# Layer 1's quartered aggregates in a two-layer graph network: where T's subtractions, the left-over banks, the running sums and the background work stand

## The chip, the cores and the metric

The kernel runs on one core of one Trainium2 chip. The metric is the device time of a whole execution in microseconds; lower is better. The times of the kernel before are 3061.73, 3063.74 and 3067.88 us, with a median of 3063.74 us.

## The reference

Two graph layers, each on 2708 nodes with 1024 features, in float32. A layer normalizes the rows, weighs every pair of nodes, masks the weights with the adjacency matrix, takes a softmax over each row and applies it to the features:

```python
h = jnp.maximum(_layernorm(x, axis=-1), 0.0)               # both layers
# layer 0
e = jax.nn.relu((h @ Wf + bf) @ (h @ Wg + bg).T)
x = x + softmax(where(adj > 0, e, NEG), axis=1) @ (h @ W + bW)
# layer 1
hw = h @ W1
e = leaky_relu(hw @ a1 + (hw @ a2).T, 0.2)
x = x + relu(softmax(where(adj > 0, e, NEG), axis=1) @ hw)
```

## The kernel before

**Panels.** The 2708 columns of the attention matrix are cut into five panels of 576, 576, 532, 512 and 512 columns (`width`). For each panel and layer, the kernel makes weights (exponentials, with a running sum `sm` over the tiles), then an *aggregate* (features times weights) and then a *project* (times W, plus the residual). Twenty tiles of 128 rows form ten pairs; one more full tile, MONO, and one of 20 rows, TINY, are left over.

**Fewer products.** Matrix products are done by a Strassen-like scheme with seven products instead of eight, named M1, M5, M6, M7, M3, M2 and M4. In layer 1, panels 1 to 4 use it twice, one inside the other (`aggregate_quartered`): the outer loop runs over the seven m in the order of `BY_QUARTERS` (M1, M5, M2, M6, M7, M3, M4), called *stages* here, and in each stage seven inner *products* follow. An inner product (`product`) is 10 matmuls, which the trace shows as 20 records, since each float32 matmul leaves two; a *pass* below is one such record. The right-hand operands are sums and differences that VectorE (DVE) makes: `make(m)` writes 20 "quarter" tiles for a stage, `fifth` writes the ten T tiles (which M5's stage uses), `second` and `fourth` rewrite the weights in place.

**PSUM banks.** A stage has the banks X, Z and Y (gx, gz, gy in the trace). The order of the products is X by M1; M4 of the stage before into that stage's Z (the closure `left_out`); Z by M6; Y by M5; X by M2; Z by M7; Y by M3. Between two products into one bank, DVE or ScalarE (ACT) has to read the bank: the second product into Z waits for `add(c12, Z, c21)`. In M2, M3 and M4 the left-over tiles follow (`left_over`, with a fourth bank U), and M7 has a *corner*, which is a `left_over` into four fresh banks. `left_over` first runs MONO's eight matmuls over all 128 rows (line 1101), then TINY's eight (line 1106). TINY's four banks use four different groups of 32 rows (`g`), with 20 rows filled in each.

**Background.** Work for later is put in lists (`later`, `lazy`) and taken up by `behind(us)`, which adds `us` to a credit and starts entries while the credit is positive. An entry of layer 1's weights is charged 2.1 us; it makes one tile of weights (ACT, two DVE operations, ACT's exponential) and adds the tile of `LAG` entries before to the sum. `exps_until(n)` forces the entries up to n. Layer 1 has 22 tiles, so there are 24 entries. The weights of the next panel are put in the list after the stage M6 and run through the rest of the aggregate and the project.

**Order.** Semaphores and the order in an engine's queue come from the framework's scheduler: an engine's instructions need not stand in the order in which they are written, except for those that are held in program order. DVE's are not held in layer 1's aggregates (`nc.hold` is empty there). Each engine then runs its own queue in order. DMA loads go through SyncE in program order.

The lines that the steps below touch: `exps, LAG` at 884, `second` in `aggregate` at 917, `quarters_of` at 1006 and after, `product` with its `behind(fine)` at 1068 to 1088, `left_over` at 1093 to 1107, `with_second`, the stage loop, and `weights1`. All DVE and ACT helpers are recorded under line 45, so their instructions are told apart by tile names: `V` or `gT` is the target of a bank's add, `T` of `fifth`, `quarter` of `make`, `P` and `sm` of the weights.

Of the kernel before, what the change touches and what calls it, by code (L numbers as in the profile page):

```python
# [57 lines left out]
def kernel(  # L58
# [155 lines left out]
    def behind(us, psum_free=False):  # L214
        credit[0] = min(credit[0] + us, 2 * us)
        while later and credit[0] > 0 and (psum_free or not later[0][3]) and (not later[0][4] or later[0][4]()):
            credit[0] -= one()
        while spare[0] and not later and lazy and credit[0] > 0:
            credit[0] -= one(lazy)
# [661 lines left out]
            nc.vector.reciprocal(r[:, o:o + w // 2], ps)  # L881
        return r

    exps, LAG = [0], 2

    def sums_until(n):
        while summed[0] < n:
# [2 lines left out]
    def exps_until(n):  # L890
        while exps[0] < n:
            one()
# [8 lines left out]
    def aggregate(l, p, S, sm, then={}, rate=3.0):  # L901
# [13 lines left out]
            sub(t1(q), wa_(q)[:, hi], wa_(q)[:, lo])  # L915

        def second():
            exps_until(2 * NQ + 2 + LAG)
            for q in range(NQ):
                sub(wa_(q)[:, hi], wb_(q)[:, hi], wa_(q)[:, hi])  # L920
            for q in range(NQ):
                sub(wa_(q)[:, lo], wb_(q)[:, hi], t1(q))
# [136 lines left out]
    def aggregate_quartered(p, S, sm, of_right, then={}, fine=1.2):  # L1059

        w = width[p]
        h = w // 2
        hb = h // 2
        lo, hi = slice(0, h), slice(h, w)
        G = both("gT")
        quad = lambda e, s: G[e].rearrange("p (c i) -> p c i", c=NH)[:, :, s]
        make, inner_right = of_right["make"], of_right["right"]
        lasts = {}  # L1070

        def product(m, n, ps, start):
            quarters_until(m)
            if (m, 0) not in lasts:
                for i, of in enumerate((hr_d[:, m, :, :, NK - 1].rearrange("p h f c -> p (h f) c"), hs2_d[:, m, :, NK - 1])):
                    lasts[m, i] = stream("hl2", (P, 4, WH))
                    load(lasts[m, i], of)
            t = stream("hc2", (P, NK - 1, WH))
            raw = n in (M1, M2, M4)
            i = {M1: 0, M2: 1, M4: 3, M6: 0, M3: 1, M7: 2, M5: 3}[n]  # L1080
            load(t, hr_d[:, m, i // 2, i % 2, :NK - 1] if raw else hs2_d[:, m, i, :NK - 1])
            last = lasts[m, int(not raw)][:, i]
            for k in range(NK):
                for d in range(2):
                    lhs = t[:, k] if k < NK - 1 else last
                    nc.tensor.matmul(ps[:, d], lhs[:, d * P:(d + 1) * P], inner_right(m, n, k),  # L1086
                                     start=(start and k == 0 and d == 0), stop=(k == NK - 1), skip_group_check=True)
            behind(fine)

        def bank2(name):  # L1090
            return bank(name)[:, :2 * hb].rearrange("p (d i) -> p d i", d=2)

        def left_over(banks, e, s, fresh):

            two = stream("hl", (P, W + 2 * P))
            load(two, hgl_d[1][:, e])
            cols = lambda b: slice(s.start + b * hb, s.start + (b + 1) * hb)
            for (a, b), ps in banks.items():
                for d in range(2):
                    c = 2 * a + d  # L1100
                    nc.tensor.matmul(ps[:, d], two[:, c * P:(c + 1) * P], S[MONO][:, cols(b)],
                                     start=((a, b) in fresh and d == 0), stop=False, skip_group_check=True)
            for d in range(2):
                for (a, b), ps in banks.items():
                    g = slice(B32 * (2 * a + b), B32 * (2 * a + b) + NY)
                    nc.tensor.matmul(ps[:, d], two[g, W + d * P:W + (d + 1) * P], S[TINY][g, cols(b)], start=False, stop=True,
                                     skip_group_check=True)

        inverse = []
        done_with = {M2: (0, lo), M7: (1, hi), M3: (0, hi), M4: (1, lo)}  # L1110

        def scale(m, r):
            if m in done_with:
                e, s = done_with[m]
                o = quad(e, s)[:, 2 * r:2 * r + 2]
                nc.vector.tensor_tensor(o, o, inverse[0][:, s].rearrange("p (o i) -> p o i", o=1).to_broadcast([P, 2, h]), OP.mult)

        place = {M1: [(1, lo)], M5: [(0, hi)], M2: [(0, lo)], M6: [(0, hi), (1, lo)], M7: [(1, hi), (1, lo)], M3: [(0, hi)],
                 M4: [(1, lo)]}
        direct = {M1: (0, lo), M5: (0, hi)}  # L1120
        more_of = {M2: (0, lo), M3: (0, hi), M4: (1, lo)}

        def into_place(m, V, r):
            for e, s in place[m]:
                o = quad(e, s)[:, 2 * r:2 * r + 2]
                if m == M1:
                    nc.scalar.copy(o, V[r])
                elif m == M5:
                    add(o, o, quad(0, lo)[:, 2 * r:2 * r + 2])
                else:  # L1130
                    add(o, V[r], o)

        def corner():

            four = {(a, b): bank2("gu") for a in range(2) for b in range(2)}
            left_over(four, 1, hi, four)
            for (a, b), ps in four.items():
                at = lambda e: quad(e, slice(h + b * hb, h + (b + 1) * hb))[:, 2 * a:2 * a + 2]
                add(at(1), ps, at(0))

        def with_second():
            exps_until(2 * NQ + 2 + LAG)
            make(M2)

        before_next = {M1: lambda: make(M5), M5: with_second, M2: lambda: (of_right["fourth"](), make(M6)), M6: lambda: make(M7),
                       M7: lambda: make(M3), M3: lambda: make(M4)}
        left_out = None
        for m in BY_QUARTERS:
            V = [quad(*direct[m])[:, 2 * r:2 * r + 2] for r in range(2)] if m in direct else [v[:, :, :h] for v in in_pairs("V")]
            c11, c12 = (V[0][:, :, b * hb:(b + 1) * hb] for b in range(2))  # L1150
            c21, c22 = (V[1][:, :, b * hb:(b + 1) * hb] for b in range(2))
            X = bank2("gx")
            product(m, M1, X, True)
            nc.scalar.copy(c21, X)
            if m == M1:
                of_right["fifth"]()
            if left_out:
                left_out()
            Z = bank2("gz")
            product(m, M6, Z, True)  # L1160
            add(c12, Z, c21)
            Y = bank2("gy")
            product(m, M5, Y, True)
            add(c22, Y, c21)
            if m == M7:
                corner()
            if m in before_next:
                before_next[m]()
            product(m, M2, X, False)
            if m not in more_of:  # L1170
                nc.scalar.copy(c11, X)
            product(m, M7, Z, False)
            add(c22, Z, c22)
            product(m, M3, Y, False)
            if m in more_of:
                U = bank2("gu")
                left_over({(0, 0): X, (0, 1): Y, (1, 0): Z, (1, 1): U}, *more_of[m], [(1, 1)])
                nc.scalar.copy(c11, X)
            add(c12, Y, c12)
            if m in more_of:  # L1180
                add(c22, U, c22)
            into_place(m, V, 0)
            scale(m, 0)

            def left_out(m=m, V=V, Z=Z, c21=c21):
                product(m, M4, Z, False)
                add(c21, Z, c21)
                into_place(m, V, 1)
                scale(m, 1)
            if m == M5:  # L1190
                of_right["second"]()
            if m == M5:
                inverse.append(inverse_sums(p, sm))
            if m in then:
                then[m]()
        left_out()
        return [t.rearrange("p (c i) -> p c i", c=NH) for t in G]

# [561 lines left out]
    def weights1(p, z, m, shift):  # L1760
# [16 lines left out]
        def go(i, mk):  # L1777
            if i < len(order):
# [13 lines left out]
                    nc.vector.scalar_tensor_tensor(s, ub[:n, :w], f[1][:n, t:t + 1], s, op0=OP.add, op1=OP.max)  # L1792
                    add(s, s, mk[0][:n, :w])
                nc.scalar.activation(s, s, AF.Exp)
            if i >= LAG:
                q, k = order[i - LAG]
                total(p, sm, S[units[q][k]], once(q, k), i == LAG)
            exps[0] += 1

        front = []  # L1800
        for i in range(len(order) + LAG):
            mk = []
            front.append([2.1, (lambda i=i, mk=mk: mk.append(load_mask(p, *order[i])))
                          if i < len(order) and not (p == 0 and units[order[i][0]][order[i][1]] in before) else None,
                          (lambda i=i, mk=mk: go(i, mk)), False, None])
# [92 lines left out]
```

## Time and profile before

| | |
|---|---|
| median of the runs | 3063.74 us (3061.73 to 3067.88) |
| the profiled execution | 3062.58 us, of which the span is 3060.8 us |
| TensorE matmuls (PE) | 2992.6 us busy, 98% of the span |
| VectorE (DVE) | 2041.7 us, 67% |
| ScalarE (ACT) | 546.0 us, 18% |
| GpSimd (POOL) | 496.2 us, 16% |
| DMA | 251 GB/s over the span |
| granted TensorE clock | 0.994 |

The span is what the instructions of the profiled execution cover. The four quartered aggregates lie at about 2333 to 2470 us (panel 1), 2532 to 2659 (panel 2), 2715 to 2837 (panel 3) and 2885 to 3007 (panel 4). A line of a timeline has the start and the length in us, the engine, the line of the kernel, the operation, target and sources, and, in brackets, the idle time before it and what ended it.

### The profile page before, as it was taken

What the parts mean: (1) busy time and instruction counts of PE and PEld (TensorE: products, weight loads), DVE (VectorE), ACT (ScalarE), POOL (GpSimd) and SP (SyncE); (2) the same over time, 40 slices, a digit from 0 to 9 for tenths busy, and PEclk for the clock granted to TensorE, in tenths of its full rate; (3) what the DMA queues carried; (4) which work ended last, traced back from release to release, by engine and by line L of the source; (5) the groups of instructions that cost most, each with busy time, mean ns of one, the idle gap of its engine ahead of it and who ended that gap; (6) DMA issues with size and microseconds to landing.
All of it is one profiled execution on the core that took longest, in us unless ns stands there. A gap on an engine that the chain in (4) does not pass through costs nothing.

```text
span 3060.8 us, 41690 instructions
## 1 busy us (share of the span) xinstructions
PE 2992.6 (98%) x14630; PEld 2293.3 (75%) x14630; DVE 2041.7 (67%) x4577; ACT 546.0 (18%) x887; POOL 496.2 (16%) x770
## 2 busy tenths in 40 slices
PE   8998999999999999999999999998999999999999
PEld 4576777657877588885888886784767959879695
DVE  5766794575741586616975266867878768887863
ACT  3420020021200121101211011202222121222200
POOL 1421111210112110214111111131212010020201
PEclk9999999999999999999999999998999999999999
DMA  6989978888466786757967588688767768878787
GB/s 228 302 257 270 300 278 304 264 270 242 158 234 157 225 248 228 246 156 243 296 196 248 165 233 274 229 294 322 249 199 254 270 204 299 285 270 295 256 302 269
DMA packets 448065, 766.80 MB, mean 251 GB/s; under 512 B 175488, under 2 KB 262304, under 8 KB 447824
## 3 DMA queue, kind: packets, MB, share of 16 engines
q1 hardware_dynamic: 387696, 584.80, 59.9%
q0 software_dynamic: 54464, 164.78, 16.2%
q10 hardware_dynamic: 5696, 14.55, 1.4%
q8 instruction: 116, 1.90, 0.2%
q14 instruction: 93, 0.76, 0.1%
HBM read 630.04 MB, written 138.11 MB: 251 GB/s over the span
## 4 chain that ended last, share of the span: by engine, by line
PE 71%; issue 11%; DVE 9%; DMA 4%; POOL 2%; SPq 1%; ACT 1%; POOLq 0%; DVEq 0%; ACTq 0%
PE gy L673 7%; PE gx L673 6%; PE gz L673 6%; PE sz L1397 6%; PE gz L1086 5%; PE pz L1286 4%; PE px L1286 4%; PE sx L1397 4%; PE sy L1397 3%; PE py L1286 3%; PE gy L1086 3%; PE gx L1086 3%; PE M_ps L586 3%; PE gv L673 2%; PE qz L673 2%
## 5 line engine op out<-in xcount | busy, mean ns | idle before, releaser
L1397 PE MATMUL sz<-B,As 128*128 128x288 f32 (+2 forms) x1200 | 292.1, 392 | 4.6 <-DVE st L45 4.5
L1397 PEld LDWEIGHTS sz<-B,As 128*128 128x128 f32 x1200 | 227.6, 190 | 53.7 <-DVE st L45 8.0
L1397 PE MATMUL sx<-B,As 128*128 128x288 f32 (+2 forms) x800 | 201.5, 395 | 14.2 <-DMA As<-hs_d 11.9
L1397 PE MATMUL sy<-B,As 128*128 128x288 f32 (+2 forms) x800 | 199.1, 392 | 0.4 <-DMA As<-hs_d 0.4
L1397 PEld LDWEIGHTS sx<-B,As 128*128 128x128 f32 x800 | 152.4, 191 | 48.4 <-DMA As<-hs_d 10.4
L673 PE MATMUL gz<-Sa,hc 128*128 128x288 f32 (+2 forms) x800 | 185.8, 392 | 0.0
L673 PEld LDWEIGHTS gz<-Sa,hc 128*128 128x128 f32 x800 | 151.5, 190 | 32.2 <-issue 1.8
L1397 PEld LDWEIGHTS sy<-B,As 128*128 128x128 f32 x800 | 151.7, 190 | 31.4 <-DMA As<-hs_d 0.9
L1086 PE MATMUL gz<-quarter,hc 128*128 128x128 f32 (+2 forms) x1344 | 168.8, 279 | 3.8 <-DVE gT L45 3.7
L1086 PEld LDWEIGHTS gz<-quarter,hc 128*128 128x128 f32 x1344 | 160.6, 191 | 5.1 <-DVE gT L45 4.5
L143 POOL DMA_DIRECT2D out_dram<-x_res x164 | 81.0, 500 | 466.9 <-DVE x_res L45 456.2
L1286 PE MATMUL py<-w,ps 128*128 128x512 f32 x320 | 142.5, 593 | 0.4 <-DMA w<-wt_d 0.4
L1286 PE MATMUL px<-w,gT 128*128 128x512 f32 x320 | 141.2, 593 | 1.5 <-ACT pt L45 1.5
L1286 PE MATMUL pz<-w,ps 128*128 128x512 f32 x320 | 142.1, 594 | 0.0
L143 POOL DMA_DIRECT2D mk_d<-mask x55 | 35.9, 653 | 511.5 <-DVE mask L45 505.4
L673 PE MATMUL gy<-T,hc 128*128 128x288 f32 (+2 forms) x480 | 113.6, 398 | 3.8 <-DMA hc<-hg_d 3.8
L1286 PEld LDWEIGHTS pz<-w,ps 128*128 128x128 f32 x320 | 60.2, 190 | 76.2 <-issue 70.3
L1286 PEld LDWEIGHTS py<-w,ps 128*128 128x128 f32 x320 | 60.4, 190 | 75.8 <-issue 72.3
L1286 PEld LDWEIGHTS px<-w,gT 128*128 128x128 f32 x320 | 60.1, 190 | 72.9 <-issue 67.1
L586 PE MATMUL M_ps<-wgT,wfT 128*128 128x512 f32 x256 | 111.8, 593 | 1.6 <-ACT hsT L45 1.6
L673 PEld LDWEIGHTS gy<-T,hc 128*128 128x128 f32 x480 | 92.2, 192 | 24.3 <-DMA hc<-hg_d 4.3
L45 ACT ACTIVATE P<-P 128x576 f32<-128x576 f32 (+2 forms) x110 | 71.9, 654 | 207.5 <-DVE P L45 207.4
(384 smaller groups left out, 5820.6 us busy)
## 6 DMA issues: line engine op xcount, KB each, us to landing
hc<-hg_d SPq DMA_DIRECT2D x175, 512.0 KB
As<-hs_d SPq DMA_DIRECT2D x150, 512.0 KB
hc<-hr_d SPq DMA_DIRECT2D x119, 512.0 KB
hc<-hs_d SPq DMA_DIRECT2D x112, 512.0 KB
w<-wt_d SPq DMA_DIRECT2D x96, 512.0 KB
w<-in_L_gnn_W_dram SPq DMA_DIRECT2D x72, 512.0 KB
md<-md_d SPq DMA_DIRECT2D x56, 512.0 KB
adj_i<-in_adj_dram SPq DMA_DIRECT2D x200, 128.0 KB
```

What stands on the lines that cost most here:

```text
L45: i = f(*a, **k)
L143: nc.gpsimd.dma_start(a, b)
L586: nc.tensor.matmul(ps, wfT[a][c // NH][:, c % NH, :], wgT[b][c], start=(c == 0), stop=(c == NC - 1))
L673: nc.tensor.matmul(ps[d], left(m, k, d), right(m, k), start=(start and k == 0), stop=(k == K - 1), skip_group_check=True)
L1086: nc.tensor.matmul(ps[:, d], lhs[:, d * P:(d + 1) * P], inner_right(m, n, k), start=(start and k == 0 and d == 0), stop=(k == NK - 1), ski ...
L1286: nc.tensor.matmul(ps, left[i][m][:, k, :], w_[k], start=(start and k == 0), stop=(k == NH - 1), skip_group_check=True)
L1397: nc.tensor.matmul(ps[:n, :h], lefts[q][:, i % 2, c, :n], B[m][c // 2][:, c % 2, :h], start=(start and c == 0), stop=(c == NH - 1), skip_g ...
```

## The change

There are four parts.

- **T's subtractions.** `of_right["fifth"]()` moves, in stage M1, from behind X's copy to behind Y's first add.
- **Bank Z last.** `left_over` handles its first three banks (MONO, then TINY), and then the fourth (MONO, then TINY). In the stages M2, M3 and M4 the fourth is Z. The corner goes through the same function and is split in the same way.
- **Sums.** In layer 1, weights are summed four entries behind instead of two (`LAG1`), so that there are 26 entries. Panel 0's plain aggregate takes part.
- **Background.** `behind(fine)` moves from the end of `product` to behind the copy or add that empties the bank, at all seven products of a stage.

```diff
-    exps, LAG = [0], 2
+    exps, LAG, LAG1 = [0], 2, 4
...
         def second():
-            exps_until(2 * NQ + 2 + LAG)
+            exps_until(2 * NQ + 2 + (LAG1 if l else LAG))
...
                     nc.tensor.matmul(ps[:, d], lhs[:, d * P:(d + 1) * P], inner_right(m, n, k),
                                      start=(start and k == 0 and d == 0), stop=(k == NK - 1), skip_group_check=True)
-            behind(fine)
...
-            for (a, b), ps in banks.items():
+            parts = list(banks.items())
+            for some in (parts[:3], parts[3:]):
+              for (a, b), ps in some:
                 for d in range(2):
                     c = 2 * a + d
                     nc.tensor.matmul(ps[:, d], two[:, c * P:(c + 1) * P], S[MONO][:, cols(b)],
                                      start=((a, b) in fresh and d == 0), stop=False, skip_group_check=True)
-            for d in range(2):
-                for (a, b), ps in banks.items():
+              for d in range(2):
+                for (a, b), ps in some:
                     g = slice(B32 * (2 * a + b), B32 * (2 * a + b) + NY)
...
         def with_second():
-            exps_until(2 * NQ + 2 + LAG)
+            exps_until(2 * NQ + 2 + LAG1)
             make(M2)
...
             nc.scalar.copy(c21, X)
-            if m == M1:
-                of_right["fifth"]()
+            behind(fine)
             if left_out:
                 left_out()
             Z = bank2("gz")
             product(m, M6, Z, True)
             add(c12, Z, c21)
+            behind(fine)
             Y = bank2("gy")
             product(m, M5, Y, True)
             add(c22, Y, c21)
+            if m == M1:
+                of_right["fifth"]()
+            behind(fine)
...
             if m not in more_of:
                 nc.scalar.copy(c11, X)
+            behind(fine)
             product(m, M7, Z, False)
             add(c22, Z, c22)
+            behind(fine)
             product(m, M3, Y, False)
             if m in more_of:
                 U = bank2("gu")
-                left_over({(0, 0): X, (0, 1): Y, (1, 0): Z, (1, 1): U}, *more_of[m], [(1, 1)])
+                left_over({(0, 0): X, (0, 1): Y, (1, 1): U, (1, 0): Z}, *more_of[m], [(1, 1)])
                 nc.scalar.copy(c11, X)
             add(c12, Y, c12)
...
             scale(m, 0)
+            behind(fine)
 
             def left_out(m=m, V=V, Z=Z, c21=c21):
                 product(m, M4, Z, False)
                 add(c21, Z, c21)
                 into_place(m, V, 1)
                 scale(m, 1)
+                behind(fine)
...
-            if i >= LAG:
-                q, k = order[i - LAG]
-                total(p, sm, S[units[q][k]], once(q, k), i == LAG)
+            if i >= LAG1:
+                q, k = order[i - LAG1]
+                total(p, sm, S[units[q][k]], once(q, k), i == LAG1)
...
-        for i in range(len(order) + LAG):
+        for i in range(len(order) + LAG1):
```

## Prediction

> **What bounds the kernel.** I read the page first: busy shares, then who waited for whom, then the queues of PE and DVE around each wait.
>
> ```profile
> span 3060.8 us, 41690 instructions
> PE 2992.6 (98%) x14630; PEld 2293.3 (75%) x14630; DVE 2041.7 (67%) x4577; ACT 546.0 (18%) x887; POOL 496.2 (16%) x770
> ...
> PE gz L1101 <- DVE V L45: 4.5, 3, 2.2
> PE gz L1086 <- DVE gT L45: 3.7, 3, 1.4
> ```
>
> PE is the bound, so time comes back only where PE stands still, and every pass added to PE is paid in full. The last two lines are the answer on waits for engine PE (total us, times, longest): they are all that PE waits in the four quartered aggregates. The change can gain little more than these 8.2 us. The first wait is in stage M3 of panels 1, 2 and 3 (2.17, 1.19 and 1.15 us in the PE timeline), where bank Z's MONO matmuls wait for the add that empties Z. The second is in stage M1 of panels 2, 3 and 4 (1.39, 1.14, 1.14), where the second product into Z waits for Z's first add. This is DVE's and PE's queue at the M1 wait of panel 2:
>
> ```profile
> 2537.84 0.42 DVE L45 TENSOR_TENSOR T<-P 128x266 f32<-128x266 f32 x1
> 2538.78 3.18 DVE L45 TENSOR_TENSOR T<-P 128x266 f32<-128x266 f32 x9
> 2541.89 0.42 DVE L45 TENSOR_TENSOR gT<-gz,gT 128x266 f32<-128x266 f32 x1
> 2543.69 0.42 DVE L45 TENSOR_TENSOR gT<-gy,gT 128x266 f32<-128x266 f32 x1
> ...
> 2551.55 3.53 DVE L45 TENSOR_TENSOR P<-P,T 128x266 f32<-128x266 f32 x10
> 2555.70 0.42 DVE L45 TENSOR_TENSOR gT<-gz,gT 128x266 f32<-128x266 f32 x1
> ...
> 2542.36 2.08 PE L1086 MATMUL gz<-quarter,hc 128*128 128x133 f32 x16 [1.39 <-DVE gT L45]
> ```
>
> All ten T subtractions stand ahead of Z's add. Note also that `second` (P<-P,T) stands ahead of adds of stage M5 that are written before it: the queue is ordered by what the scheduler takes to be ready, not as written. Now the left-over matmuls, PE's timeline in panel 3, stages M2 and M7:
>
> ```profile
> 2760.90 0.37 PE L1106 MATMUL gx<-P,hl 20*128 20x128 f32 x1
> 2760.91 0.37 PE L1106 MATMUL gy<-P,hl 20*128 20x128 f32 x1
> 2760.91 0.37 PE L1106 MATMUL gz<-P,hl 20*128 20x128 f32 x1
> 2760.92 0.37 PE L1106 MATMUL gu<-P,hl 20*128 20x128 f32 x1
> 2761.11 0.27 PE L1106 MATMUL gx<-P,hl 20*128 20x128 f32 x1
> ...
> 2787.49 1.95 PE L1101 MATMUL gu<-P,hl 128*128 128x128 f32 x16
> 2789.37 0.73 PE L1106 MATMUL gu<-P,hl 20*128 20x128 f32 x16
> 2790.03 2.05 PE L1086 MATMUL gx<-P,hc 128*128 128x128 f32 x16
> ...
> 2792.36 1.95 PE L1086 MATMUL gz<-quarter,hc 128*128 128x128 f32 x16
> ```
>
> TINY's passes start four at a time, one per bank: 16 records take the time of four steps.
>
> **What the Trainium skill says.** The page "TensorE: Matmul & The Clock Gate", section "The mechanism" under packing small matmuls, says that matmuls in different row groups run at once, some 4 ns apart, while matmuls otherwise keep their order; the trace agrees (2760.90 to 2760.92). Its section "Why this matters for your kernels" says that a single matmul of 32 rows takes as long as one of 128; no row here shows one alone. The page "TensorEngine Tiling (Array Packing)", section "Key Properties", says that a change of tiling mode drains TensorE; the trace agrees in that a TINY block takes twice its four steps (below).
>
> **Part by part.**
>
> *Z last, the cost.* A pass of panel 3 lasts 0.1115 us (a product of 20 starts each 2.23 us in PE's timeline). The corner's MONO matmuls start at 2787.49 and 16 passes end at 2789.27. The product after TINY has a successor that starts at 2792.36, so it runs in effect from 2790.13. TINY costs 0.86 us: 0.45 for four steps and 0.41 for going into and out of the small tiles. The same working gives 0.90 in panel 1 (corner: 2414.82 plus 1.96, against 2420.13 less 2.45) and 0.87 in panel 2 (M3: 2637.04 plus 0.45, against 2640.63 less 2.27); panel 4 has panel 3's width. After the change X, Y and U still share four steps, and Z has two matmuls, four passes, in one row group with nothing beside them. Between lie Z's MONO passes on the full array. So each `left_over` has two TINY blocks instead of one, and each block goes in and out. Calls: M2, M3, M4 and the corner in four panels, 16 (line 1106 has 256 records, 16 a call). Sum: 4 x (0.90 + 0.87 + 0.86 + 0.86) = 14.0 us, all on PE. Bounds: if going in and out were free, four passes each, 4 x (0.49 + 0.45 + 0.45 + 0.45) = 7.3 us; that a block's passes can't load weights ahead is excluded, since one bank's own passes follow each other by 0.11 to 0.12 after the first. I take 14.0, because the second block has the same neighbours (full array on both sides) as the one measured.
>
> *Z last, the gain.* In M3, Z's MONO passes move behind U's four passes and the first TINY block: 0.45 + 0.86 = 1.3 us later (1.4 in panel 1). That covers 1.19 and 1.15, and 1.4 of 2.17.
>
> *Background behind the adds.* The same number of calls of `behind`, so the same work. In panel 1, two weight entries stood between the last `quarter` subtraction and Z's add (DVE from 2439.28 to 2444.99), each with a wait of 0.71 for ACT's exponential. One entry is about 2.9 us with its wait; if one goes behind the add, the rest of the 2.17 is gone. I take the three M3 waits as gone: 4.5 us, plus 0.1 at each restart (2636.48 to 2637.04 is 0.56 for four passes that take 0.45): 4.8. Moved entries delay nothing on PE: their readers come stages later, and DVE is busy 116.24 of 148 us in the densest window (2330 to 2478). No DMA is added; the entries' mask loads on SyncE and the hook's fetches keep their order among each other, moved by less than one product.
>
> *T behind the adds.* In panel 2 the first add of Y starts at 2543.69, and later adds follow at 2.4 us a product (two products to 2548.59, one to 2551.00). That spacing is the scheduler's idea of when banks are full. By it Z's add has its place at 2543.7 - 2.4 = 2541.3; it stood at 2541.89. So T delayed it by about 0.6 us; the rest of the place is the scheduler's, which will fill the time before with T again, as it filled it with `second`. Panels 3 (2721.85 against 2721.3) and 4 (2894.86 against 2894.3) give 0.6 and 0.5. Gain 1.7 us. Bounds: nothing, if T stays; all 3.7 and 0.3 for restarts, 4.0, if the add comes as soon as Z is full. T's readers don't become late: Y's bank is full at 2538.54 (the next product starts), so ten T subtractions of 0.35 behind its add would end near 2543 even with none hoisted, and `make(M5)`, 20 of about 0.21, near 2547.5. M5's first product reads T from 2545.6 and its product into Z reads the quarters from 2550.2 (2547.00 and 2551.54, less the 1.39).
>
> *Sums four behind.* 22 totals of 0.7 us as before; two entries more with a total alone. DVE waited for ACT's exponential 17.6 us in 27 pieces between 2325 and 3061 ("DVE sm" on "ACT P"), and most of that goes. DVE isn't the bound, so I count it at nothing beyond its help in M3. If the cover is missing, the two entries come later by their charge of 4.2 us and put two totals, 1.4 us, into stage M1; this could push Z's add, and I keep it in the range. Panel 0's aggregate shows no wait on weights.
>
> *Sum.* 14.0 - 4.8 - 1.7 = 7.5 us. The profiled execution took 3062.6 (span 3060.8), which gives 3070.1; it lies 1.2 under the median of the runs, from which it would be 3071.2. I say 3070.5.
>
> **Rivals.**
> - *All six waits go.* The scheduler puts Z's add at once: 14.0 - 8.8 = 5.2, so 3067.8. For it: the change names the very instructions. Against: hoisted `second`.
> - *Waits stay or move.* If DVE's queue is refilled so that as much is waited for as before, only the TINY blocks count: 3076.6. For it: readiness rules the queue, and the new totals fall in M1. Against: in M3 Z's passes themselves come later.
> - *Not slower.* Z's lone TINY block is cheap, because its weights are loaded ahead and the full array closes up behind it: 7.3 - 8.8 = -1.5, so 3061.1 if all waits go as well. It decides where a second block costs under 8.8 / 16 = 0.55 us. For it: nothing here shows a lone block. Against: the measured block spends 0.41 us beyond its passes, in all three widths. Further down it can't go, since four passes have to run.
>
> **How the numbers follow.** Forecast 50%, all waits gone 20%, waits stay 18%, not slower 12%. A measurement here can tell about 0.2%, 6.1 us, from no change. Slower by that: 0.36 of the forecast, 0.05 of the second, 0.17 of the third, 0.58. Faster: 0.05 of the last case and 0.01 of the rest, 0.06. Within: 0.36. The range 3063.5 to 3076.5 holds the first two cases, half of the third and little of the last, 8 in 10.
>
> **What would show it.** Line 1106 with the same 256 records, but its busy time, 11.85 us in the window 2330 to 3030, near 23; Z's four passes alone some 0.11 apart. No wait of gz on DVE V in M3; waits of gz on DVE gT in M1 smaller, not gone, with some T still ahead of the add. DVE's waits on ACT P far below 17.6. I am wrong if a second block takes under 0.55 us, or if a wait appears in M5 on T or quarter.

## The result and the profile after

The changed kernel takes 3092.05 us (median, 3086.95 to 3096.24) against 3064.14 us for the kernel before in the same comparison. The ratio is 1.0095 with a 95% interval of 1.0083 to 1.0107: some 28 to 29 us slower. The prediction had 3070.5 us, from 7.5 us on top of the profiled execution of before.

These lines of the page after answer to the first two shown of before:

```profile
span 3087.9 us, 41693 instructions
PE 3016.3 (98%) x14630; PEld 2313.3 (75%) x14630; DVE 2042.0 (66%) x4577; ACT 545.1 (18%) x887; POOL 495.9 (16%) x770
```

The work is the same, pass for pass, and PE is busy 23.7 us longer. The waits of PE in the aggregates, after (total us, times, longest):

```profile
PE gy L1086 <- DVE V L45: 10.5, 3, 3.6
PE gz L1086 <- DVE gT L45: 2.9, 4, 1.0
```

Z's waits in stage M3 are gone, as predicted, and those in M1 are smaller. But there is a new wait, of bank Y on its add, in stage M3 of panels 1 to 3. It is larger than all the waits of before together.

To compare kernels I use one stretch: from the start of the first quartered aggregate to the start of the last project, from PE's timelines (2333.01 to 3007.34 before, 674.33 us; 2334.59 to 3034.46 after, 699.87 us). It grew by 25.5 us; the projects between take the same 61.8, 52.9 and 48.1 us in both. The four aggregates grew by 6.34, 7.43, 8.55 and 3.22 us. The two spans differ by 27.1 us; the other 1.6 us lie ahead of the stretch. That front part takes 2331.55 to 2343.16 us in the kernels below, though little or nothing is changed in it, while the projects inside the stretch agree within 0.01 us in all of them. So the stretch is the steadier measure.

The waiting instruction, in PE's timeline after, stage M3 of panel 1:

```profile
2438.16 2.12 PE L1086 MATMUL gx<-P,hc 128*128 128x144 f32 x16
...
2446.57 3.01 PE L1086 MATMUL gy<-P,hc 128*128 128x144 f32 x16 [3.35 <-DVE V L45]
2449.37 1.17 PE L1086 MATMUL gy<-P,hl 128*128 128x144 f32 x4
```

Bank Y was full at 2438.16, where X's product starts. Y's second product starts only at 2446.57. Note also its own length: 3.01 and 1.17, where the product before took 2.12 and 0.65. First the wait. DVE's queue at this place, before:

```profile
2436.17 0.45 DVE L45 TENSOR_TENSOR V<-gy,V 128x288 f32<-128x288 f32 x1
...
2438.72 0.64 DVE L45 TENSOR_TENSOR quarter<-T,quarter 128x144 f32<-128x144 f32 x2
2439.28 0.77 DVE L45 SCALAR_TENSOR_TENSOR P<-ub,f,P 128x532 f32<-128x532 f32 x1
```

and after:

```profile
2443.93 0.29 DVE L45 TENSOR_TENSOR quarter<-T,quarter 128x144 f32<-128x144 f32 x1
2444.15 0.76 DVE L45 SCALAR_TENSOR_TENSOR P<-ub,f,P 128x532 f32<-128x532 f32 x1
...
2446.08 0.44 DVE L45 TENSOR_TENSOR V<-gy,V 128x288 f32<-128x288 f32 x1
```

Before, Y's add stood amid the twenty `quarter` subtractions of `make(M4)`, 2.11 us behind Z's first add of the stage (2434.06). After, it stands behind all twenty and behind five operations of weights and sums as well, 7.98 us behind Z's add (2438.10). It is written ahead of `make(M4)` in both kernels.

Then the matmul's length. Here are stretches of 3.41 us after, with the busy time of PE, PEld, DVE, ACT and POOL, the granted clock, the DMA share and GB/s:

```profile
2444.45:2447.86 3.41, 1.29 (x10) 1.29 (x11) 3.07 (x6) 1.27 (x2) 0.00 (x0) 1.00 0.31 126
2447.86:2451.28 3.42, 3.42 (x16) 3.42 (x15) 2.20 (x4) 0.65 (x1) 0.00 (x0) 0.50 0.20 25
2451.28:2454.69 3.41, 3.41 (x31) 2.83 (x31) 1.49 (x3) 0.40 (x1) 0.00 (x0) 1.00 0.74 282
```

After the wait, TensorE's clock in the records is 0.50 for one such stretch, and half as many passes get through (16 against 31). The same happens in panel 2 (one stretch) and panel 3 (two). At half the clock, half of PE's time is lost: 1.7 us in panels 1 and 2, and in panel 3, where PE works at half clock from 2830.92 to 2836.99, 3.0 us, 6.4 us in all. So a wait is dearer than it looks: 10.5 us of waiting drew 6.4 us of slow running, which the page shows as busy time.

Last, the split blocks, in PE's timeline after (stage M2 of panel 1):

```profile
2386.12 0.39 PE L1107 MATMUL gx<-P,hl 20*128 20x144 f32 x1
...
2386.61 0.28 PE L1107 MATMUL gu<-P,hl 20*128 20x144 f32 x1
2386.82 0.76 PE L1102 MATMUL gz<-P,hl 128*128 128x144 f32 x4
2387.51 0.75 PE L1107 MATMUL gz<-P,hl 20*128 20x144 f32 x4
2388.19 0.77 PE L865 MATMUL mx_ps<-ident,mx 128*128 128x128 f32 x5
```

Three banks start together, then Z's MONO, then Z's four TINY passes alone. From X's first MONO pass (2384.56) to line 865 are 3.63 us; before, the same took 2.76 us. The difference is 0.87, where the prediction had 0.90. The block of three banks takes 0.70 us from its first start to Z's MONO, and Z's lone block takes 0.68 us to line 865: a block costs as much with one bank as with three.

### The profile page after: what moved, and what is told of

Read it like the earlier page. It is cut to its first block, busy times and chain, and to the rows that moved or that the text cites. A ratio compares the mean times of both kernels' runs of the same rounds, so it can differ in the third digit from the quotient of the medians.

```text
span 3087.9 us, 41693 instructions
## 1 busy us (share of the span) xinstructions
PE 3016.3 (98%) x14630; PEld 2313.3 (75%) x14630; DVE 2042.0 (66%) x4577; ACT 545.1 (18%) x887; POOL 495.9 (16%) x770
## 4 chain that ended last, share of the span: by engine, by line
PE 75%; issue 11%; DVE 8%; DMA 3%; POOL 2%; SPq 1%; ACT 1%; POOLq 0%; DVEq 0%; ACTq 0%
PE gy L673 7%; PE gz L673 6%; PE gx L673 6%; PE gz L1086 6%; PE sz L1405 5%; PE pz L1294 4%; PE px L1294 4%; PE gy L1086 4%; PE gx L1086 3%; PE sx L1405 3%; PE sy L1405 3%; PE py L1294 3%; PE M_ps L586 3%; PE gv L673 3%; PE qz L673 2%
```

## The experiments

All these kernels compute the whole result. "Region" is the change of the 674.33 us above, in one profiled execution of each kernel. One stretch at half clock more or less in it, 1.7 us, may be chance of that execution (last section).

| | ratio to before, 95% | region, us |
|---|---|---|
| the change | 1.0095 [1.0083, 1.0107] | +25.5 |
| 1 background alone | 1.0039 [1.0027, 1.0051] | +9.3 |
| 2 Z last, split, alone | 1.0026 [1.0017, 1.0036] | +8.5 |
| 3 sums alone | 1.0019 [1.0011, 1.0027] | +4.1 |
| 4 T alone | 1.0011 [1.0003, 1.0019] | +1.7 |
| 5 the change, Y's add held | 1.0112 [1.0095, 1.0129] | +32.9 |
| 6 Z last, TINY blocks adjoining | 0.9997 [0.9987, 1.0007] | −1.5 |
| 7 background at one product | 1.0006 [1.0000, 1.0013] | +2.4 |
| 8 no background at two of M3's products | 1.0006 [0.9997, 1.0014] | +2.0 |
| 9 the change without the split | 1.0029 [1.0019, 1.0039] | +11.9 |
| 10 the change without background | 1.0041 [1.0028, 1.0054] | +14.0 |
| 11 adds first | 0.9981 [0.9973, 0.9989] | −4.5 |
| 12 adds first, background at X | 1.0019 [1.0012, 1.0026] | +7.4 |
| 13 the change without sums | 1.0065 [1.0052, 1.0078] | +22.3 |
| 14 adds first, an entry less | 0.9967 [0.9954, 0.9980] | −5.9 |

My theory after the result: the background's place sends Y's add behind `make(M4)`, and the split costs what was predicted. The rivals: the sums do it, or the two together.

### One part at a time

**1. Background behind the adds, alone.** `behind(fine)` out of `product`, and behind the copy or add at all seven products; the rest as before.

> The kernel before with the background alone moved behind the adds. Two-costs theory (the split left-over block costs 14 us; the background's new place lets Y's add in stage M3 fall behind the making of M4's quarters, three waits of 10.5 us and 6.5 us of matmuls at half clock after them): those 17 us come here, less the 4.8 of the M3 waits on Z, so about +12 us (3076), with PE waiting for DVE V at gy in panels 1 to 3 and no second TINY block. Rival (the sums four behind fill DVE's queue and push Y's add): no gy wait, 0 to -5 us. Rival (the split changes what PE and DVE do in M3): the same, 0 to -5.

The region grew by 9.3 us. The wait of gy on DVE V appears (8.6 us, three times), and DVE's queue in M3 has the changed kernel's order. Two of the three waits (2.96 and 2.92) are followed by half clock, the first (2.69) isn't. This part makes Y's wait by itself.

**2. Bank Z last with the split, alone.**

> The kernel before with bank Z last in the left-over work alone, as the change has it. Two-costs theory: +14.0 for sixteen second TINY blocks, -4.8 for the M3 waits, +9 us (3073), no wait at gy, line of TINY's matmuls busy about 23 us. Rival (the split also delays Y's add): +26. Rival of the prediction (a lone block is cheap): under +3.

The region grew by 8.5 us. No wait of gy; Z's waits in M3 fell from 4.5 to 0.2 us. Taking back those 4.3 us and 0.1 at each of three restarts gives about 13 us for 16 second blocks. TINY's busy time is that of the whole change, 23.27 us.

**3. Sums four behind, alone.** `LAG1 = 4` in layer 1.

> The kernel before with the sums four behind alone. Two-costs theory: within 3 us of before, DVE's waits on ACT's exponential (17.6 us from layer 1's first panel on) less than half, no gy wait. Rival (the sums push Y's add): +12 us or more, with the gy waits.

The region grew by 4.1 us: −2.15 in panel 1, where M3's wait on Z is gone, and +3.19 and +3.07 in panels 2 and 3. There, in PE's timeline (panel 2, M3 and the stage after):

```profile
2635.88 0.72 PE L1101 MATMUL gz<-P,hl 128*128 128x133 f32 x4 [2.76 <-DVE V L45]
...
2637.68 3.68 PE L1086 MATMUL gx<-T,hc 128*128 128x133 f32 x16
```

The wait was 1.19 before, so 1.57 more; and the next sixteen passes take 3.68 instead of 1.98, at half clock. 1.57 + 1.70 = 3.3, the 3.19 measured. DVE's wait of sums on ACT's exponentials stays at 17.6 us (26 times): what the change of lag was expected to take away, it doesn't.

**4. T's subtractions, alone.**

> The kernel before with T's subtractions alone moved behind the first adds. All theories: -1 us, as the M1 waits at gz on DVE gT fall from 3.7 us to about 2.7; -4 if the adds came as soon as Z is full; + if M5 waits for T.

M1's waits fell from 3.7 to 2.9 us, but the region grew by 1.7 us, all in panel 1 (+1.69). M3's wait on Z there is 2.19, as it was before (2.17), and this time a half-clock stretch of 3.42 us follows it, which none did in the kernel before. Panels 2 to 4 are unchanged within 0.06 us. Aligned product by product, panel 4 shows where its gain goes: Z's second product in M1 starts 0.32 us earlier against the start of the aggregate, and so do the next products; in stage M5 the lead falls to 0.28, 0.17 and 0.06, and there it stays. Moving T alone wins nothing, since what T's later place takes comes back a stage later, in pieces mostly too small for a wait's line. The 1.7 us are the clock's, and may be chance: the wait stands at the same place of the aggregate as before (112.5 us from its start) and is as long. The ratio, 1.0011 and clear of 1, leaves open whether part of it lasts.

The four parts sum to 23.5 us of 25.5.

### What makes Y late

**5. The change, with Y's add kept in its written place.** `held` keeps the DVE instructions of its calls in written order.

```diff
-            add(c22, Y, c21)
+            held(add, c22, Y, c21)
...
-                before_next[m]()
+                held(before_next[m])
```

> The whole change, with Y's first add and the quarters that are made behind it kept in the written order on DVE. If the order of these two on DVE's queue is what costs the 17 us (waits at gy and half clock): the gy waits are gone, and the split blocks are left, 14 less 4.8 less 1, about +8 against before (3074). If gy waits for something else (the clock, a bank, a load): as the change, about +27.

It is slower still, +32.9 us. Gy's wait is gone, and a bigger one stands in its place (waits of PE):

```profile
PE gz L1102 <- DVE V L45: 15.8, 3, 5.4
```

Now Z's add in M3 comes behind `make(M4)` and the weight work. Each half-clock stretch is 10.24 us long. My forecast missed. What is short in M3 is DVE's time: twenty subtractions and some weight entries stand between the bank adds, and the order decides which bank pays and how much.

**7. Background moved at one product only,** M6 into Z.

```diff
-            behind(fine)
+            if not (n == M6):
+                behind(fine)
...
             add(c12, Z, c21)
+            behind(fine)
```

> The kernel before with the background moved behind the add at one of the seven products alone, the first into Z (M6). If this place alone puts Y's add behind the making of M4's quarters: gy waits of about 3 us in panels 1 to 3 and +9 us as in the kernel with all seven moved. If it takes several places: no gy waits, 0 to +2.

The region grew by 2.4 us. Y waits in the same three places, but 1.4 us at most (4.0 in all), and no half clock follows. One place is enough for the whole new order: between Z's first add and Y's in M3 stand the same twenty subtractions and five operations as in the changed kernel, 7.98 us in panel 1 in both. The difference is when DVE comes to M3. Z's add there starts 2.18 us before X's product here, 0.72 us before it in kernel 1, with all seven places, and 0.06 us before it in the changed kernel. Y waits 1.24, 2.69 and 3.35 us: wait and lead add up to 3.41 or 3.42 us in each. Panel 4, where no weights are left to make, keeps the old order and has no such wait in any of these kernels.

**10. The change without its background part.**

> The whole change without its background part: behind(fine) stays at the end of product. If the background's place is what pushes Y's add behind make(M4) in stage M3, the gy wait and the half clock behind it are gone, and what is left is the split and the sums: about 8.5 + 4.1 + 1.7 - 1 (M3's waits on Z are covered by the split), 11 to 14 us over the kernel before in the region. Rival: the sums four behind alone also make Y's add late once Z is last; then gy on DVE V stays, at 3 us or more in all.

+14.0 us, as the theory had it. Waits of PE on bank adds in M3:

```profile
PE gz L1103 <- DVE V L45: 2.7, 2, 1.5
```

No gy. So within the whole change it is the background's place that makes Y late, and it costs 25.5 − 14.0 = 11.6 us there. The waits it makes are dearer (16.9 us with the clock), but without it Z waits again in M3: 2.7 us, and two half-clock stretches in panel 3.

**13. The change without its sums part.**

> The whole change without its sums part: weights summed two entries behind. The order of DVE's queue in stage M3 is the whole change's: all twenty quarter subtractions, two entries, then Y's add. If that order is what costs, the wait of gy stays near 10 us in three panels with the half clock behind it, and the region of the four aggregates is within 2 us of the whole change's 25.5. Rival: the sums cost inside the whole what they cost alone, 4.1 us; then the region is near 21.5.

+22.3 us; nearer to the rival's 21.5 than to within 2 us of 25.5. But gy still waits, 8.6 us, behind the same queue, so the sums don't make that wait. With them DVE comes to M3 later (in panel 1 its lead over X's product is 0.72 us without them and 0.06 with them). That adds 1.9 us to the wait, and 1.3 by the clock, since panel 3 has one half-clock stretch here instead of two.

### What the split costs

**6. Z last, with the two TINY blocks next to each other.** All MONO passes first, then TINY of three banks, then TINY of Z.

```diff
-            for d in range(2):
-                for (a, b), ps in banks.items():
+            for some in (parts[:3], parts[3:]):
+              for d in range(2):
+                for (a, b), ps in some:
```

> The kernel before with bank Z last, all MONO matmuls first, then TINY's three banks, then TINY's fourth: a second TINY block without passes on the full array between. If half of a second block's 0.86 us is going into and out of small tiles: only its passes are left, 0.33 to 0.45 a call, 16 calls, +5 to +7, less 1.5 as Z comes 0.5 us later in three panels: about +4. If passes alone in one row group cost what the block costs: +12.

Panel 4, which has no waits in M3, grew by 0.09 us for four calls: 0.02 a call instead of 0.86. I had expected more. The trace shows why: there is no second block. In PE's timeline, panel 4, Z's passes run in step with the others:

```profile
2935.81 0.37 PE L1109 MATMUL gx<-P,hl 20*128 20x128 f32 x1
...
2935.85 0.37 PE L1109 MATMUL gz<-P,hl 20*128 20x128 f32 x1
...
2936.02 0.27 PE L1109 MATMUL gx<-P,hl 20*128 20x128 f32 x1
```

Z's first pass starts 0.04 us after X's first and ahead of X's second, in all 16 calls, although it is written behind both of X's matmuls. So this kernel doesn't price a second block without full-array passes between. It shows that Z's passes are nearly free when nothing parts them from the others, so that in the split it is the MONO passes between the blocks that make them dear. Whether PE's queue held them in this order or PE took them ahead, the trace doesn't tell.

**9. The change without the split.** Z comes last, but MONO of all four banks and then TINY of all four.

> The whole change, but bank Z only comes last in left_over: all MONO matmuls of the four banks, then all TINY matmuls of the four banks together, as before. If the second TINY block between full-array passes is a pure toll on TensorE, the time falls by 13.7 us from the changed kernel's, and TINY's busy time goes back from 23 to about 12 us; the wait of gy on DVE in stage M3 stays at about 10 us, with the clock's fall behind it, and the region of the four aggregates ends up some 12 us over the kernel before. Rival: the second block also covers for Z's late add in M3, since it comes at the end of DVE's pile there; then a wait of gz on DVE V comes back, 1 to 2 us in each of three panels, and less than 10 us are won.

+11.9 us, where 12 was expected, and TINY's busy time is back. This is the row of line 1107, from 2330 to 3040 (length, PE, PEld, granted clock, DMA share, GB/s), in this kernel:

```profile
2330.00:3040.00 710.00, 11.85 (x256) 8.68 (x256) 0.99 0.81 274
```

and in the changed kernel:

```profile
2330.00:3040.00 710.00, 23.27 (x256) 16.93 (x256) 0.99 0.80 268
```

The split costs 25.5 − 11.9 = 13.7 us in the whole change. By panels it is 3.5, 3.4, 3.5 and 3.3. Gy's wait is as in the whole change (10.5 us), so the second block hid nothing.

### Towards a faster kernel

**8. Fewer entries in M3.** No background at the products M2 and M7 of stage M3. Z comes last with all TINY together. In M1, Z's and Y's adds and then `fifth` are held in that order.

> The kernel before, with its waits taken away in another way: no background at two products of stage M3 (X by M2, Z by M7), Z last with one TINY block for all four banks, and in stage M1 the two first adds and then T kept in the written order on DVE. If the six waits are worth what they show: no gz waits, 8.8 us less, 0.9971. If the entries left out come back as waits elsewhere, or quarters become late in M5: 0 or more.

+2.0 us. All of Z's waits are gone, and another has come, of X on ACT: 2.31, 2.02 and 2.06 us in stage M1 of panels 2 to 4, with half clock behind each. PE's timeline, panel 2:

```profile
2537.12 3.17 PE L1086 MATMUL gx<-P,hc 128*128 128x133 f32 x16 [2.31 <-ACT gT L45]
```

ACT's:

```profile
2536.15 0.65 ACT L45 ACTIVATE P<-P 128x532 f32<-128x532 f32 x1 [1.59 <-DVE P L45]
2536.70 0.36 ACT L45 COPY gT<-gx 128x266 f32<-128x266 f32 x1
```

The entries left out of M3 are made around M1, and X's copy stands on ACT behind an exponential that itself waits for DVE. Panel 1, whose M1 has no such entries, is 2.44 us shorter.

**11. Adds first.** As kernel 8, with all background where it was before. This is the core of it:

```diff
-            if m == M1:
-                of_right["fifth"]()
...
-            add(c12, Z, c21)
+            (held if m == M1 else lambda f, *a: f(*a))(add, c12, Z, c21)
...
-            add(c22, Y, c21)
+            if m == M1:
+                held(add, c22, Y, c21)
+                held(of_right["fifth"])
+            else:
+                add(c22, Y, c21)
...
-                left_over({(0, 0): X, (0, 1): Y, (1, 0): Z, (1, 1): U}, *more_of[m], [(1, 1)])
+                left_over({(0, 0): X, (0, 1): Y, (1, 1): U, (1, 0): Z}, *more_of[m], [(1, 1)])
```

> Built on the kernel before: bank Z last in left_over with all TINY matmuls together, and in stage M1 Z's and Y's first adds and then fifth held in program order on DVE; background and sums as before. If the adds' places in DVE's queue are all that the waits hang on, M1's waits of gz on DVE gT (3.7) go with 0.1 at each restart, 4.0, and M3's waits shrink by the four passes, 0.45 each, 1.3: 5 us less than the kernel before. Rival: DVE's work has to be done anyway, and T or make(M5) comes late; then a wait in stage M5 or of gx, gz in M1's later products takes the place, and the time is within 2 us of the kernel before.

−4.5 us and a ratio of 0.9981: faster than both kernels. DVE's queue in M1 of panel 2:

```profile
2539.40 0.42 DVE L45 TENSOR_TENSOR gT<-gz,gT 128x266 f32<-128x266 f32 x1
2539.75 0.41 DVE L45 TENSOR_TENSOR gT<-gy,gT 128x266 f32<-128x266 f32 x1
2540.09 3.53 DVE L45 TENSOR_TENSOR T<-P 128x266 f32<-128x266 f32 x10
```

Both adds stand ahead of all ten T now, M1's waits are gone, and nothing waits for T or `quarter` in M5. In M3, Z still waits 1.70, 0.74 and 0.71 us (3.2 in all). In panel 1 a half-clock stretch follows, which eats 1.7 us, so that panel alone is longer than before, by 1.2 us.

**12. Adds first, with background moved at product M1 into X.**

> As the adds-first kernel, and background moved behind the copy at product M1 into X only, not behind an add. DVE's order in M3 then has the entries earlier in the aggregate. If that place is free, the same time as the adds-first kernel within 1.5 us, and M3's waits of gz on DVE V under 3 us. Rival: ACT's exponentials get ahead of X's copy, as in the kernel without background in M3; then gx waits on ACT, 2 us or more in each of three panels, and the gain is lost.

+7.4 us; both forecasts missed. X doesn't wait. Z waits in M3 (8.4 us, 2.8 in each panel), with half clock behind every one. In DVE's queue two weight entries, instead of one, now stand together just ahead of the last add of stage M7, and in panel 1 the first add of M3 comes at 2437.54 (2433.83 in kernel 11, whose aggregate starts 0.8 us earlier): DVE enters M3 late.

**14. Adds first, and one entry less in M3.**

```diff
-            behind(fine)
+            if not (m == M3 and n in (M7,)):
+                behind(fine)
```

> As the adds-first kernel, and no background at product M7 of stage M3, so that one weight entry stands ahead of Z's add there instead of two. If the entries are what makes Z's add late in M3, gz's wait on DVE V (3.2 us) and the half clock in panel 1 (1.7 us) are gone, and the region is 4 us shorter than the adds-first kernel's 669.80. Rival: the entry that is left out is made in the project or at the next stage M1, where X's copy on ACT stands behind its exponential; then gx waits on ACT in panels 2 to 4, 2 us each with half clock behind it, and the region is no shorter.

The lowest ratio of all, 0.9967 [0.9954, 0.9980], 3057.73 us against 3067.49. The interval overlaps kernel 11's, so that the runs don't show which of the two is faster. Its waits of PE:

```profile
PE gz L1086 <- DVE gT L45: 3.0, 4, 0.9
```

M3's waits are gone, and there is no half clock anywhere in the region. X doesn't wait on ACT. In exchange the weight work that was pushed out of M3 ends later, and Z's and Y's adds, T and the quarters of M1 stand behind it (panel 2: Z's add at 2541.63, 2539.40 in kernel 11, whose aggregate starts 0.6 us earlier). The delay shows in panels 2 to 4 where M1's last product goes into Z behind Z's second add (0.83, 0.82 and 0.89 us), and in panel 4 at Z's first add too (0.47). That is 3.0 us in all, so that the region is 1.4 us shorter than kernel 11's and not 4. The region explains 5.9 of the 9.8 us between the medians. The interval begins at 6 us, and what goes beyond the region isn't explained.

## Where the prediction was right and where wrong

**The split, 14.0: right.** 13.7 by leaving it out of the whole change, 0.87 for one call. The rival that a lone block is cheap falls: Z's block alone takes as long as that of three banks. (Four passes each would have made 7.4 us in its bound, not 7.3.)

**M3's waits on Z, −4.8: right in place, worth less.** They are gone, and the split alone takes them from 4.5 to 0.2 us (kernel 2). But in the whole change more DVE work than before stands ahead of Y's add, and Y's wait is over twice what Z's were.

**T, −1.7: about −0.1 in each panel at most.** The waits fell from 3.7 to 2.9 us: one of ten T moved behind Z's add, 0.33 us a wait. But "T's readers don't become late" failed by that much; stage M5 gave it back. In panel 4, without the split (kernel 9), 0.10 is left of it.

**Sums, nothing: wrong for the part alone.** +4.1 us alone and 3.2 us within the whole, through later adds in M3; the prediction had put its worry into M1. DVE's waits of sums on ACT P are 14.8 us (23 times) after, not far below 17.6, and its waits of weights on ACT P grew from 6.5 to 14.4 us (7 times each).

**Background, nothing: the step that failed.** "Moved entries delay nothing on PE: their readers come stages later, and DVE is busy 116.24 of 148 us in the densest window." The two reasons stand, but the conclusion doesn't follow from them. The readers of the entries aren't the question. What matters is who stands behind them in DVE's queue, and the average over 148 us says nothing of the 7.98 us in M3 between Z's add and Y's. The prediction had itself noted that the queue is ordered by readiness and not as written, and used this for T and in a rival, not for Y's add. The moved background made the wait of gy, 3.35 + 3.61 + 3.54 = 10.5 us, of which the sums add 1.9 (kernel 13); leaving this part out of the whole change saves 11.6 us of the region (kernel 10).

**The clock: absent from the sum.** 6.4 us behind these waits. With the 10.5 that makes 16.9 of the 18.0 us by which the region missed the forecast (25.5 less 7.5); T's shortfall is 1.6 and the split's excess −0.3, which closes the sum within 0.2. The rival "Waits stay or move" pointed the right way with 3076.6, but it held that as much would be waited for as before, 8.2 us; it is 13.4, and 6.4 of slow clock.

What stays open is why the scheduler puts Y's add behind `make(M4)` when background is written behind the adds. The runs show that it does, that one place suffices, and that it happens only in panels where weights are still being made; the reason inside the scheduler wasn't looked into.

## What to carry to other kernels

Moving work that an engine does in a filled stretch moves the wait to whoever is behind it: ask of the stretch, not of the average, how much time the engine has, and list its queue there, all banks, before counting a moved step at nothing. Where a scheduler reorders, "behind the add" in the text is not behind the add in the queue; hold the few instructions that PE waits for, and leave the rest. In M1 that won (kernel 11); in M3, where DVE has no time to spare, it moved the wait to the next bank (kernel 5), and taking work out helped (kernel 14). And price a wait of more than about 1.5 us of a busy TensorE with what the clock may take after it.

## What the runs showed of the hardware

The clock's falls follow a fixed grid. In eleven of these kernels there are 25 falls in the region; each lasts 3.40 to 3.42, 6.80 to 6.84 or 10.24 us. Within a kernel, the starts lie whole multiples of 3.413 us apart (after: 2447.86, 2645.84 and 2830.16, which are 58.0 and 112.0 steps). In the stretch of 3.41 us that ends where the clock falls, PE was busy between 0.14 and 1.92 us. In the regions of all sixteen traces, no stretch of the grid with 2.00 us or more at full clock was followed by a fall. So the share of a fixed window decides, and not the length of a wait: a wait of 2.19 us was followed by a fall in kernel 4, one of 2.69 was not in kernel 1, where the grid cut it in two.

Between 1.4 and 1.92 us it matters whether the window holds TINY's passes. All that fell with 1.42 us or more held some; two without any, with 1.65 us (kernel 1) and 1.79 us (the kernel before, at the wait of panel 1), didn't fall. The latter, with the grid carried on from falls elsewhere in its trace:

```profile
2441.53:2444.94 3.41, 1.79 (x15) 1.58 (x13) 2.66 (x4) 1.22 (x2) 0.00 (x0) 1.00 0.78 257
```

A window that is slow and again not filled stays slow for another: 2.65 us busy in panel 3 after, and up to 2.97 elsewhere, where windows with 3.17 us or more recovered. Three slow windows with PE busy throughout stayed slow too (kernels 5 and 10), and each held Z's lone TINY block. That such passes count for less fits all this, but no kernel was made to try it.

Executions of one kernel differ in the clock they are granted. Of 124 of the kernel before, the six with a mean clock of 0.991 took 3072.7 us on average, the 28 with 0.994 took 3063.9 us. A grid that lies differently against the same waits each time would do this; only one execution of each kernel has a trace, so it isn't shown.

The Trainium skill's page "TensorE: Matmul & The Clock Gate", section "What's actually happening", describes such a window, 3413 ns long and free-running. The traces agree, to the second decimal. Its section "Why this matters for your kernels" asks for no idle gaps over some 3 us. Here a wait of 1.54 us next to TINY's passes was enough (kernel 10, panel 3), so that the measured share of the window is the safer guide: falls up to 56% busy (1.92 us), none from 2.00 us on.
